# A decoder layer with routed experts: logits with experts on partitions, two shared blocks moved, scatters one by one

## The chip, the cores and the metric

The kernel runs on one core of a Trainium2 chip. The metric is the time on the device in microseconds, the median over the runs shown; lower is better. Beside it there is one execution with a profile, from which all durations of single instructions come. The core has five engines with a queue of instructions each: TensorE (PE; PEld is its weight load), VectorE (DVE), ScalarE (ACT), GpSimd (POOL) and SyncE (SP), which here only issues transfers. Each queue is worked off in order. Transfers run on 16 DMA engines.

## The reference

One decoder layer on x of 8 batches x 512 tokens x 256 features, in 32-bit floats, each part on the layer-normed x and added to x:

```python
x = x + _L0_attn_ref(_layernorm(x), W_A, W_V, W_O, b_O)          # 16 heads; a softmax over the tokens, applied as a causal convolution
x = x + _L0_xattn_ref(_layernorm(x), ctx_1024, ctx_1024, WK, WV, WQ)   # one causal head: softmax(Q K' / 16) V; K from x's norm, V and Q from ctx
x = x + _L0_ffn_ref(_layernorm(x), router_w, wg_r, wu_r, wd_r, wg_s, wu_s, wd_s)

# in _L0_ffn_ref, for each token t:
out = einsum(silu(t wg_s) * (t wu_s), wd_s)          # 2 shared experts, 128 wide
logits = flat @ router_w                             # 16 experts
weights, indices = top_k(softmax(logits), 2)         # weights scaled to sum 1
out = out + sum over the 2 chosen of weight * (silu(t wg_r) * (t wu_r)) wd_r    # routed experts, 64 wide
```

(The second part's arguments come in the order keys, values, queries.)

## The kernel before, in words

**Batches.** The loop over `b` handles one batch of 512 tokens at a time. Each batch has a front (`steps_front`: first norm, the token softmax `zsoft`, values, the context's queries and values), a back (`steps_back`: convolution `conv` and `summed`, output projection `proj`, second norm, `scores`, `probsT`, `attend`, third norm, router) and a shared block (`steps_shared`: two `hidden` with gate and up matmuls, two `down`). All are lists of small functions. `merged` (line 46) lays several lists over each other by the fraction of each list that a step stands at. In batch b run the back of b, the shared block of b-1 and the front of b+1.

**Order.** The order in which steps are called is the program order, and gives priorities. A planner then orders each engine's instructions, and puts a later one first where it expects the earlier to wait. So the trace shows the token column of batch 0's row tile (line 511) at 8.3 us, long before that batch's router. Tiles have tags with a fixed number of buffers (`bufs`); a tile waits until a buffer of its tag is free.

**Routing.** `router` (line 440) takes the transposed normed x (`x2T`) as the stationary operand against `wr_sb` with 16 columns, so that tokens lie on partitions and 16 logits beside each other, and VectorE finds the two best experts. `ranked` (line 487) counts tokens per expert with two matmuls and gives each a `place` in a table `xg` in DRAM; it also sets column 0 of the row tiles (line 511) to the number of the token's result row, r * n + token, where n is the number of tokens in the group. `send` (line 523) scatters the rows with indirect DMAs from GpSimd, 8 per batch of 129 KB. The tag `row` has two buffers, one for each of the two choices, so the next batch's row tiles wait for these scatters.

**Groups.** Batches 0 to 4 are group 0, batches 5 to 7 group 1. When a group's last batch is ranked, SyncE writes 17 blank blocks into `xg` (line 518), `tiled` and `tabled` make a table of row tiles, and the routed work (`steps_routed`) goes by four tiles of 128 rows, called q here: 14 q for group 0, 10 for group 1. For each q: `fetch` loads rows (`xs`) and down weights (`wdn`, two buffers) with register addresses on SyncE, `pick` copies gate and up weights on ScalarE, `turn` transposes the rows on TensorE (line 676), `hidden` (line 695) and `down` (line 709) are the expert, and its results `y`, weighted on ScalarE and VectorE (lines 720, 722), are scattered at once to `yg` by four indirect DMAs on GpSimd (line 723). GpSimd also does the small power of each layer norm (line 196).

Group 0's list of 72 steps is cut in three, 30, 30 and 12, laid over batches 5, 6 and 7. Group 1's list (`late`) runs after the batches, with the joins of group 0 laid over it. The shared block's end stores x as `kept` in DRAM (line 575); `keep`, `take` and `join` load it and the two result rows of each token (`yj`) back, add them (line 775) and store the output.

After batch 7's merged steps, router, `down` of block 6, `ranked`, the shared block of batch 7 and the sends come in a list written out by hand (line 810). The weight product `qk_sb` (wq times wk, line 159) is made before anything else on TensorE.

## Time and profile before

| | us |
|---|---|
| runs without profile | 666.7, 681.52, 676.43; median 676.43 |
| profiled execution, its own time | 669.43 |
| its span, first to last instruction | 667.7 |
| TensorE busy | 548.0 (82%) |
| VectorE busy | 376.3 (56%) |
| GpSimd busy | 227.8 (34%) |
| ScalarE busy | 187.6 (28%) |
| DMA moved | 109.77 MB, mean 164 GB/s |

The work stands in the trace as follows: batch 0 until about 90 us, then about 51 us a batch; batch 5 from 297 to 384, batch 6 to 474, batch 7 to 528 and its routing to 545; group 1's tiles from 564 to 638; scatters, joins and stores until the end. Busy time is summed over these stages, and a stage's own limit can differ from that of the whole. A wait line reads: engine and its waiting instruction, what released it, then total time, how often, and the longest. A timeline line reads: start, duration, engine, line, operation, output and inputs, count, and in brackets the engine's idle time before it with its releaser.

### The profile page before, as it was taken

Reading aid. Unit: us, or ns where it says so; the run is one execution under the profiler, and the core shown is the slowest. Engines: PE = TensorE matmul, PEld = TensorE weight load, DVE = VectorE, ACT = ScalarE, POOL = GpSimd, SP = SyncE. Lnnn points to the kernel's source line nnn. Section 1 sums busy time; section 2 is a strip of 40 time slices with the busy share of each in tenths; the row PEclk is TensorE's granted clock in tenths of the full one; section 3 lists DMA queues with packets and bytes.
Section 4 is the critical chain, followed back from the end, with each engine's and each line's share of the span. In section 5 each row is a group of like instructions: output and inputs, shape, how many; then the busy total and the mean of one; then the engine's idle time right before and its main releaser. Section 6 shows DMA issues by size and latency. Waiting matters only on the chain.

```text
span 667.7 us, 9943 instructions
## 1 busy us (share of the span) xinstructions
PE 548.0 (82%) x3132; PEld 346.1 (52%) x3132; DVE 376.3 (56%) x1213; ACT 187.6 (28%) x459; POOL 227.8 (34%) x257
## 2 busy tenths in 40 slices
PE   4879978998998998994999988999988881877820
PEld 2435624655655665552657645567565641654610
DVE  5156637668668658766455547554765481334424
ACT  2213212322322322312343332433422101433210
POOL 3011142125125125215033374325453521246560
PEclk9999988999999999999799998999989795979775
DMA  7562610631721631636338642286522077677879
GB/s 261 193 251 76 242 65 31 234 124 49 254 103 57 223 127 65 208 141 204 114 83 263 229 135 83 71 266 200 162 83 81 1 231 228 185 230 235 245 232 312
DMA packets 71397, 109.77 MB, mean 164 GB/s; under 512 B 9219, under 2 KB 45837, under 8 KB 70800
## 3 DMA queue, kind: packets, MB, share of 16 engines
q1 hardware_dynamic: 63664, 92.27, 43.0%
q0 software_dynamic: 7680, 16.87, 7.1%
q8 instruction: 25, 0.41, 0.3%
q14 instruction: 28, 0.23, 0.1%
HBM read 83.40 MB, written 35.43 MB: 178 GB/s over the span
## 4 chain that ended last, share of the span: by engine, by line
PE 46%; DMA 14%; DVE 12%; issue 10%; SPq 7%; POOL 7%; ACT 2%; POOLq 1%; DVEq 0%; ACTq 0%
DMA xs<-xg 5%; PE pa L419 4%; PE psc L390 4%; PE pt L212 4%; PE pv L306 3%; PE pv L276 3%; PE pq L294 3%; PE pgu L695 3%; PE pc L338 3%; PE pg L553 3%; POOL xg L527 3%; SPq L518 3%; POOL yg L723 2%; PE pz L244 2%; POOL rs L196 2%
## 5 line engine op out<-in xcount | busy, mean ns | idle before, releaser
L723 POOL DMA_INDIRECT yg<-y,to x96 | 97.7, 1018 | 113.8 <-ACT y L720 89.4
L196 POOL TENSOR_TENSOR rs<-ve,power 128x2 f32<-128x2 f32 x48 | 34.4, 723 | 167.0 <-DVE ve L195 166.9
L527 POOL DMA_INDIRECT xg<-row,place x64 | 63.1, 986 | 78.2 <-DVE place L510 50.6
L695 PE MATMUL pgu<-xsT,wgu 128*64 128x128 f32 x768 | 67.6, 316 | 7.5 <-ACT xsT L679 6.4
L695 PEld LDWEIGHTS pgu<-xsT,wgu 128*64 128x64 f32 x768 | 51.6, 158 | 23.7 <-issue 12.6
L676 PE MATMUL pxt<-ident,xs 128*128 128x128 f32 x192 | 37.6, 308 | 29.3 <-DMA xs<-xg 28.3
L338 PE MATMUL pc<-T,vh 128*32 128x256 f32 (+1 forms) x512 | 53.2, 493 | 9.0 <-DVE late L354 6.6
L676 PEld LDWEIGHTS pxt<-ident,xs 128*128 128x128 f32 x192 | 21.5, 148 | 49.7 <-DMA xs<-xg 30.2
L419 PE MATMUL pa<-v,pT 128*128 128x256 f32 x160 | 40.7, 385 | 2.8 <-DVE pT L410 2.8
L181 DVE BATCH_NORM_STATS2 bn<-x 128x6 f32<-128x256 f32 x96 | 38.0, 418 | 8.7 <-DMA x<-in_x_dram 7.6
L390 PE MATMUL psc<-kT,qT 128*128 128x128 f32 (+3 forms) x128 | 42.1, 460 | 0.5 <-ACT kT L215 0.5
L709 PE MATMUL py<-wdn,rh 64*128 64x256 f32 x192 | 37.5, 428 | 5.1 <-DVE h L557 4.7
L372 PE MATMUL po<-wo_sb,oT 128*128 128x256 f32 x128 | 35.1, 407 | 5.9 <-DVE oT L357 3.2
L200 DVE TENSOR_SCALAR xn<-x,mv,rs 128x256 f32<-128x256 f32 x64 | 26.5, 440 | 21.6 <-POOL rs L196 19.5
L212 PE MATMUL pt<-ident,xn 128*128 128x128 f32 x128 | 26.1, 302 | 15.1 <-DVE xn L200 11.6
L338 PEld LDWEIGHTS pc<-T,vh 128*32 128x32 f32 x512 | 16.3, 109 | 40.0 <-issue 24.5
L698 DVE SCALAR_TENSOR_TENSOR rh<-rh,pgu 128x256 f32<-128x256 f32 x24 | 10.0, 418 | 46.9 <-ACT rh L697 46.9
L663 ACT COPY wgu<-wgu_r 128x256 f32 x96 | 32.2, 401 | 11.6 <-DVE col L637 9.2
L570 PE MATMUL pd<-wd_sb,h 128*128 128x256 f32 x128 | 34.9, 411 | 0.5 <-DVE h L558 0.5
L306 PE MATMUL pv<-xwv_sb,ctxT 128*128 128x256 f32 x128 | 34.7, 392 | 0.0
L419 PEld LDWEIGHTS pa<-v,pT 128*128 128x128 f32 x160 | 29.2, 190 | 10.4 <-issue 3.7
L372 PEld LDWEIGHTS po<-wo_sb,oT 128*128 128x128 f32 x128 | 23.5, 197 | 20.7 <-issue 6.5
(156 smaller groups left out, 949.7 us busy)
## 6 DMA issues: line engine op xcount, KB each, us to landing
T<-zd SPq DMA_DIRECT2D x32, 1024.0 KB
xs<-xg SPq DMA_DIRECT2D x96, 129.0 KB
wdn<-wdn_d SPq DMA_DIRECT2D x96, 64.0 KB
xg<-blank SPq DMA_DIRECT2D x34, 129.0 KB
x<-in_x_dram SPq DMA_DIRECT2D x8, 512.0 KB
ctxT<-in_ctxT_dram SPq DMA_DIRECT2D x8, 512.0 KB
kept<-x SPq DMA_DIRECT2D x8, 512.0 KB
xj<-kept SPq DMA_DIRECT2D x8, 512.0 KB
```

The lines of the kernel that those rows point to most:

```text
L181: nc.vector.bn_stats(stats["bn"][:, c, :], src[:, c, :])
L196: nc.gpsimd.tensor_tensor(stats["rs"][:, lo:hi], ve[:, lo:hi], power[:, lo:hi], ALU.pow)
L212: nc.tensor.transpose(pt[:, i * P:(i + 1) * P], xn[:, k * P:(k + 1) * P], ident)
L306: nc.tensor.matmul(pv[:, i, :], s["ctxT"][:, k, j * P:(j + 1) * P], xwv_sb[:, k, :], start=(k == 0), stop=(k == KC - 1))
L338: nc.tensor.matmul(s["pc"][o][32 * g:32 * g + 32, 2 * jp * P:], v_bufs[b % 2][:, jp, h, :], s["T"][h // HPT][:, h % HPT, :S - 2 * jp * P], ...
L372: nc.tensor.matmul(po[:, i, :], s["oT"][:, k, c * P:(c + 1) * P], wo_sb[:, k, :], start=(k == 0), stop=(k == KC - 1))
L390: nc.tensor.matmul(pc[:, :w], s["qT"][:, k, i * P:w], s["kT"][:, k, :w], start=(k == 0), stop=(k == KC - 1))
L419: nc.tensor.matmul(pa[:, :D], s["pT", i][:, j * P:(j + 1) * P], s["v2"][:, j, :], start=(j == 0), stop=(j == i))
L527: ins = nc.gpsimd.indirect_dma_start(out=grp[g]["xg"][:, :], out_offset=bass.IndirectOffsetOnAxis(ap=s["place"][:, r, c:c + 1], axis=0), i ...
L676: nc.tensor.transpose(pt[:, i * P:(i + 1) * P], xs[:, i, 2 + k * P:2 + (k + 1) * P], ident)
L695: nc.tensor.matmul(p[o * MR:(o + 1) * MR, n, j, :], wgu[:, i, n, k, :], xT[:, k, i, :], start=(k == 0), stop=(k == KC - 1))
L723: ins = nc.gpsimd.indirect_dma_start(out=G["yg"][:, :], out_offset=bass.IndirectOffsetOnAxis(ap=G["to", q][:, i:i + 1], axis=0), in_=y[i], ...
```

## The change

The logits are made by a step `logits` of its own: `wr_sb`, padded with zeros to 32 columns, is stationary, and each group of 128 tokens goes to its own 32 partitions of the result. ScalarE copies it, and `router` transposes it back. `make_qk` moves behind batch 0's values. Shared block 5 moves whole from batch 6 to batch 7, and the two `hidden` of block 6 move to later places in batch 7. Group 0's list is spaced with empty steps (`idle`), and the scatters are steps of their own (`put`), one at a time between the other steps and two q later than the tile's `hidden`; group 1 scatters right after `down` as before. The list is now 152 steps, cut 72, 54, 26. The hand-written list at the end is in a new order, with the loads `keeps` and `takes` before `ranked`. Group 1's x is no longer stored in DRAM: it stays in its three buffers of tag `x`, and group 0's `keep` uses the buffers of `ctxT` and `oT` instead. The tags `xT`, `to` and `y` have 5, 4 and 8 buffers in place of 4, 3 and 5.

```diff
+def idle(n):
+    return [lambda: None] * n
...
-    wr_sb = load("wr_sb", wr, [P, KC, NE])
+    wr_sb = const.tile([P, KC, 32], F32, name="wr_sb")
+    nc.gpsimd.memset(wr_sb, 0.0)
+    nc.sync.dma_start(out=wr_sb[:, :, :NE], in_=wr)
...
-    for m in range(KC):
-        pq = ps.tile([P, 512], F32, tag="mm", bufs=3, name=f"pqk{m}")
...
+    def make_qk():
+        for m in range(KC):
+            pq = ps.tile([P, 512], F32, tag="mm", bufs=3, name=f"pqk{m}")
...
+        if b == 0:
+            steps.append(make_qk)
         steps += [queries(0), queries(1), context_values(0), context_values(1), bias]
...
+        def logits():
+            pl = ps.tile([P, 512], F32, tag="mm", bufs=3, name=f"pl{b}")
+            for k in range(KC):
+                for c in range(NT):
+                    nc.tensor.matmul(pl[32 * c:32 * c + 32, :P], wr_sb[:, k, :], s["x2T"][:, k, c * P:(c + 1) * P], start=(k == 0), stop=(k == KC - 1))
+            s["lT"] = sb.tile([P, P], F32, tag="lT", bufs=1, name=f"lT{b}")
+            nc.scalar.copy(s["lT"], pl[:, :P])
+
         def router():
-            pl = ps.tile([P, 512], F32, tag="mm", bufs=3, name=f"pl{b}")
-            pl3 = pl[:, :NT * NE].rearrange("p (c e) -> p c e", e=NE)
-            for c in range(NT):
-                for k in range(KC):
-                    nc.tensor.matmul(pl3[:, c, :], s["x2T"][:, k, c * P:(c + 1) * P], wr_sb[:, k, :], start=(k == 0), stop=(k == KC - 1))
+            pl = ps.tile([P, 512], F32, tag="tr", bufs=2, name=f"plt{b}")
+            nc.tensor.transpose(pl[:, :P], s["lT"], ident)
+            pl3 = pl[:, :P].rearrange("p (c e) -> p c e", e=32)[:, :, :NE]
...
-        steps += [router, ranked, send(0), send(1)]
+        steps += [logits, router, ranked, send(0), send(1)]
...
-                if cp == 1:
+                if cp == 1 and where[b][0] == 0:
                     s["kept"] = dram.tile([P, NT, D], F32, tag="kept", bufs=B, name=f"kept{b}")
...
-                        ins = nc.gpsimd.indirect_dma_start(
...
+                G["y", q] = y
+            return f
+
+        def put(q, i):
+            def f():
+                ins = nc.gpsimd.indirect_dma_start(
...
+            return f
...
-        steps += [lambda: tiled(g), lambda: tabled(g), fetch(0), fetch(1), pick(0), fetch(2), turn(0)] + [fetch(3)] * g
-        for q in range(nq + 1):
-            if q + 1 < nq:
-                steps += [pick(q + 1), turn(q + 1)]
-            if q < nq:
-                steps.append(hidden(q))
-            if q + 3 + g < nq:
-                steps.append(fetch(q + 3 + g))
-            if q > 0:
+        steps += [lambda: tiled(g), *idle(0 if g else 4), lambda: tabled(g), fetch(0), fetch(1), pick(0), fetch(2)]
+        steps += [fetch(3)] if g else idle(12)
+        steps.append(turn(0))
+        for q in range(nq + 2):
+
+            puts = [put(q - 2, i) for i in range(QT)] if g == 0 and q > 1 else idle(QT)
+            steps += [pick(q + 1), puts[0], turn(q + 1)] if q + 1 < nq else [puts[0]]
+            steps += [puts[1], hidden(q)] if q < nq else [puts[1]]
+            steps += [puts[2], fetch(q + 3 + g)] if q + 3 + g < nq else [puts[2]]
+            steps.append(puts[3])
+            if 0 < q <= nq:
                 steps.append(down(q - 1))
+                if g:
+                    steps += [put(q - 1, i) for i in (0, 2, 1, 3)]
...
-                x = sb.tile([P, NT, D], F32, tag="x", bufs=3, name=f"xj{b}")
+                x = sb.tile([P, NT, D], F32, tag=("ctxT", "oT")[bi % 2], bufs=1, name=f"xj{b}")
...
-                x, y = G["xj", bi], G["yj", bi]
+                x, y = G["xj", bi] if g == 0 else st[b]["x"], G["yj", bi]
...
-    n = len(routed) // 7
-    routed = [routed[:3 * n], routed[3 * n:6 * n], routed[6 * n:]]
+    first = [f for f in routed]
+    n = (len(first) - 18) // 14
+    routed = {5: first[:18 + 6 * n], 6: first[18 + 6 * n:18 + 12 * n], 7: first[18 + 12 * n:]}
+    shared = [steps_shared(b) for b in range(B)]
...
-        if b > 0:
-            now.append(steps_shared(b - 1))
+        if 0 < b < 6:
+            now.append(shared[b - 1])
...
-        if b >= 5:
-            now.append(routed[b - 5])
+        if b in routed:
+            now.append(routed[b])
         if b == B - 1:
 
-            router, ranked, *send = now[0][-4:]
-            hidden, down = now[1][:NSH], now[1][NSH:]
-            now[:2] = now[0][:-4], hidden
+            logits, router, ranked, *send = now[0][-5:]
+            now[0] = now[0][:-5]
+            now += [shared[5] + idle(3), idle(3) + shared[6][:NSH]]
...
-    for f in [router, *down, ranked, hidden[0], *send, late[0], keeps[0], takes[0], keeps[1], takes[1], hidden[1], late[1], *rest]:
+    for f in [logits, down6[0], router, keeps[0], takes[0], keeps[1], takes[1], down6[1], ranked, hidden7[0], *send, late[0], hidden7[1], late[1], *down7]:
         f()
     old = [joins[0], keeps[2], takes[2], joins[1], keeps[3], takes[3], joins[2], keeps[4], takes[4], joins[3], joins[4]]
-    keeps, takes, joins = steps_join(1)
-    for f in merged(late[2:], old):
+    _, takes, joins = steps_join(1)
+    for f in merged(late[2:], old + idle(4)):
         f()
-    for f in [*keeps, *takes, *joins]:
+    for f in [*takes, *joins]:
         f()
```

## The prediction

> **What bounds the kernel now.** I read the page first, then TensorE's waits between the batches' borders, then the timelines around the longest of them, then the chain after the last batch. From the page, busy tenths and granted clock in slices of 16.7 us, and one cost group:
>
> ```profile
> PE   4879978998998998994999988999988881877820
> ...
> PEclk9999988999999999999799998999989795979775
> ...
> L723 POOL DMA_INDIRECT yg<-y,to x96 | 97.7, 1018 | 113.8 <-ACT y L720 89.4
> ```
>
> TensorE is at 9 tenths in the batches, so a batch costs what TensorE has to do plus what it waits. Full waits are few. TensorE's waits in 295 to 320 us (batch 5 starts), 385 to 475 (batch 6) and 475 to 545 (batch 7):
>
> ```profile
> PE pxt L676 <- DMA xs<-xg: 6.1, 1, 6.1
> ...
> PE py L709 <- DVE h L557: 4.7, 1, 4.7
> ...
> PE pa L419 <- DVE pT L410: 2.8, 1, 2.8
> PE pt L212 <- DVE row L200: 2.2, 1, 2.2
> PE po L372 <- DVE oT L357: 2.0, 1, 2.0
> ```
>
> The first is the first transpose of routed rows, reached before its rows are. The other four lead to GpSimd. Its timeline at 390 us, and VectorE's:
>
> ```profile
> 389.10 0.97 POOL L723 DMA_INDIRECT yg<-y,to  x1 [0.31 <-DVE late L354]
> 390.38 0.96 POOL L527 DMA_INDIRECT xg<-row,place  x1 [0.30 <-DVE late L356]
> ...
> 399.21 0.96 POOL L527 DMA_INDIRECT xg<-row,place  x1 [0.30 <-issue]
> 400.18 0.73 POOL L196 TENSOR_TENSOR rs<-ve,power 128x2 f32<-128x2 f32 x1
> ...
> 400.95 0.73 DVE L200 TENSOR_SCALAR xn<-x,mv,rs 128x256 f32<-128x256 f32 x2 [8.78 <-POOL rs L196]
> ```
>
> Twelve scatters of about 1.27 us stand ahead of a layer norm's small power. VectorE waits 8.78 us for it, and the `h` of L557 that TensorE wants is queued behind. VectorE also stalls where the token column of the next row tile (L511) waits for the last batch's sends:
>
> ```profile
> 92.17 0.17 DVE L511 TENSOR_SCALAR row<-tok 128x4 f32<-128x4 f32 x1 [6.83 <-DMA xg<-row,place]
> ```
>
> After 545 us batches no longer count. The windows view gives TensorE 4.35 us of work in 545 to 565, and none after 638.3. The chain there runs blank rows, fetches on SyncE, scatters, loads of `yj`, two adds and the store.
>
> **The change, part by part** (against the span of 667.7 us; the execution's own time is 669.43, so 1.7 lie outside).
>
> 1. *`make_qk` goes behind the first values.* Now its 3.46 us (7.84 to 11.3) precede the first transposes, whose inputs are ready at 7.2 to 7.8: up to 3.5 us for the softmax chain. But TensorE waits only from 26.6 to 28.9 for `T` and 2.3 us more at 29 to 31, and the matmuls must still run before the queries. VectorE's wait for x1 until 11.8 can keep part. -2, from +0.5 to -3.5. The memset ahead of `wr_sb`'s load is hidden: GpSimd ends its constants at 2.3 us, that DMA is issued at 6.8.
>
> 2. *Logits.* Now 16 records per batch (L445) take 135.41 to 136.22, 137.67 to 137.89 and 138.40 to 139.02, together 1.65 us. After: 16 records moving 128 columns. The nearest row is L695 (128 columns, 64 wide), 32 records in 1.90 us, so 0.95; the transpose is 2 records of L212's kind (4 in 0.44), 0.22. TensorE saves 0.5 a batch. Against this stands the Trainium skill, "TensorEngine Tiling (Array Packing)", section "Restrictions": tiling by columns gives up the fast weight load. If the 16 loads then ran one after another at 109 ns (the row of L338, 128x32) it would be 1.75 us plus the transpose, 0.3 more than now instead of 0.5 less, 6.4 us over eight batches. L338 itself argues against: such tiles stream 48 records in 4.08 us (at 297.5), 85 ns each, below their 109 ns load, so the loads overlap. I take -0.5.
>  The added wait: copy on ScalarE (128x256 is 0.37, 128x128 about 0.3), transpose 0.2, and two handovers, some 0.2 each by the gaps between L212 and L215: VectorE starts the router about 1 us later, and `ranked`, the sends and L511 with it. Queued behind L511 are `late`, `oT` and TensorE's `po`. Five borders show that stall. The transposed logits also hold one of two `tr` buffers until the router's subtraction, 0.5 us. Eight times -0.5 is -4; five times +1 is +5: +1, from -4 to +8 (the transpose queued behind other matmuls, rival C).
>
> 3. *Head of group 0 in batch 5.* Twelve empty steps put `turn(0)` at 22.5/72 of the batch instead of 6.5/30: 0.10 of 87 us, 8 us later, more than the 6.1 us waited. The attention of batch 5 fills the place. The cold clock behind the wait goes too. In rows: 8 `pxt` in 2.17 us (1.04 at 482 us), 4 `pt` 1.12 (0.60), 32 `pgu` 3.68 (1.97), 4 `pg` 2.12 (1.88) sum to 3.6 us lost; the windows view gives a clock of 0.51 from 317.2 to 325. The Trainium skill, "TensorE: Matmul & The Clock Gate", section "Part 1: The HAM clock gate", allows one window of about 3.4 us at half rate after an idle one, a loss of 1.7. By the rule this part is worth 7.8, by the rows 9.7, because the clock stayed low over twice that time. Rows decide; but six tiles now turn in batch 5 instead of five, over less of it, and a fetch may be awaited again (now 2.2 us). -8, from -2 to -10.
>
> 4. *Scatters one by one, two tiles late; shared blocks.* 24 and 20 scatters stay at 1.27 us each. What goes is GpSimd waiting for `y` (89.4 us in the group above), and four in a row ahead of a power. The eight sends stay in a row, but start when `place` is ready (387 instead of 390.4; 477.2 instead of 480.1), so L196, L511 and their followers come 3 us or more earlier. Of the waits 4.7 + 2.8 + 2.2 + 2.0 = 11.7 I take -8, from 0 to -11.7. The moved blocks are neutral in work: 16 gate/up and 16 down records (4 in 1.72, 8 in 1.73 us) of block 5 leave batch 6 for batch 7, 10.3 us (block 6's gate and up are there already), and one routed tile of about 5 us moves ahead over each of the borders 5/6 and 6/7. They cost where tag `h` has three buffers: both `h` of block 5 now are held at 1.5/7 when `summed(1)` at 5.5/24 wants two. The shuffle then waits for `down` of block 5, and `oT`, `proj` and the attention of batch 7 behind it. TensorE has the 7 us of the block itself and routed tiles to do meanwhile: +2, from 0 to +6. A fifth `xT` buffer and eight `y` buffers cost only space.
>
> 5. *Dispatch of group 1.* From the first router step (531.49) to `both` (539.5) VectorE takes 8.2 us; in batch 1 5.1 (139.20 to 144.3). Between them stand two adds of `down` with waits of 0.56 and 1.61. These go around the router now: -3, and +1 for the longer logits. The loads of `keeps` and `takes` go ahead of `ranked`, so beside 17 blank loads (11.2 us of SyncE) there is no `yj` and no `kept` store; the last blank's 5.62 us of landing should come nearer 4.6 as in group 0: -1. Together -3, from -5 to +1.
>
> 6. *Late tiles, 564 to 638.* Ten tiles at 7.4 us. `wdn` has two buffers, so SyncE issues tile q's only when `py` of q-2 is done (576.46, issue at 576.48), then `xs` of q+1 (1.9), which lands in some 3 us, and that sets `py` of q. Old joins sit in this queue: out 0.59, xj 0.58, two yj 1.2. By step positions there are ten instead of nine ahead of the last fetch, and `keep` 4 reuses the buffer of join 2 just ahead of it: +0.6 and up to a landing of 3, less contention: +2, from -3 to +7.
>
> 7. *End.* No `xj` loads for group 1 (issued at 634.7, 642.8 and 649.8) and joins of group 0 over earlier: a scatter took 7.33 us to land at 633, 2.1 later, and held the next by 1.5; 512 KB at 262 GB/s is 2 us beside the `yj` loads. -3, from 0 to -5.
>
> Sum: -2 + 1 - 8 - 8 + 2 - 3 + 2 - 3 = -19: span 648.7, execution 650.4. The median shown is 676.43/669.43 = 1.0105 times the profiled one: 657.
>
> **Rivals.**
> *B, waits move.* Removing one stall exposes the next: VectorE and the fetches also have gaps in batches 5 to 7 (`xs` is awaited at 363 and 421 in the chain), so half of part 3 and a third of part 4 come through: -2 + 1 - 4 - 3 + 2 - 1 + 2 - 2 = -7, 660.7, median 669. For: nearly every wait of VectorE there is short and has another behind it. Against: TensorE is at 0.93 to 0.96 in those batches, so it has work ready.
> *C, slower: the transpose of the logits waits in TensorE's queue behind shared gate and up* (3.8 us, at 139.5 to 143.1 just there now). Seven borders at 3.8 are 27, and 2 more at the last: -19 + 29 = +10, 677.7, median 686. It decides from 19/7 = 2.7 us of extra delay per border. Against: the planner places these fillers where it expects a wait, so it may as well place the transpose first.
> *D, more:* all waits of parts 3 and 4 and the late contention go: 644.
>
> **Numbers.** Forecast 0.55 (650 to 664), B 0.25, C 0.10, D 0.10. Runs of before spread from 666.7 to 681.5, so 2% (662.9) is what can be told from no change. Faster: 0.48 + 0.03 + 0.09 = 0.60; slower: half of C, whose median lies just inside 2%, and a remainder, 0.05 + 0.04 = 0.09; same 0.31. The range reaches to B's upper and D's near end: 644 to 678, leaving out most of C and the far half of D.
>
> **What would show it.** First `pxt` with no wait and clock 1.0 from 310 to 340 (3); no L200 waiting over 3 us for L196 in batches 6 and 7 (4); first transposes near 8 us and `T` issued before 22 (1); L511's waits longer by about 1 us in batches 1 to 4 (2); 32 us from the first router step of batch 7 to the first late `pgu`, now 35.1 (531.49 to 566.61) (5); tiles of 7.4 to 7.7 us (6); at most 27 us from last `py` to end, now 29.4 (7). I am wrong if the router's chain lengthens by over 2 us a batch, or if batch 6 keeps its 90 us without its shared block.

## The result and the profile after

The changed kernel takes 679.86 us (median of 20 runs, 674.14 to 684.23). The kernel before, run beside it on the same chip, takes 674.46 us. The ratio is 1.010, with a 95% interval from 1.0067 to 1.0133: a little slower, where 657 us and "faster" were forecast. The profiled execution of after is near the slow end of its runs (span 681.0 us) and that of before near the fast end of its own (667.7), so the two profiles differ by 13.3 us where the medians differ by 5.4. So sizes of totals are taken from the ratios, and a stage of a single profile is read with care: e10, e11, e12 and e15 differ only in batches 5 to 7, and their batch 0 takes 81.4 to 84.3 us, their batches 1 to 4 together 214.5 to 218.1.

From the page of after, the busy tenths and the clock in slices of 17.0 us, and the costliest group:

```profile
PE   4878978999899889899799897999989780687930
...
PEclk9999989999899899799799997989979985788575
...
L746 POOL DMA_INDIRECT yg<-y,to x96 | 95.4, 994 | 113.8 <-ACT y L738 87.3
```

TensorE is as full as before. What stands out is the last line: the wait of GpSimd for `y`, which was to go when the scatters became steps of their own, is 87.3 us; it was 89.4 (line 723 of the kernel before). The clock row has lost a tenth or two in several places of the first half.

Where the time lies is read by stages. Stage b0 runs from the start to the first count matmul (`pk`) of batch 0, and a stage b1 to b7 from the first `pk` of the batch before to the first `pk` of its own. "Dispatch" goes from batch 7's `pk` to the first transpose of group 1's rows, "late" to the end of the last `py`, and "end" to the end of the span. All rows of this table are profiles from chips on which before takes 674 to 675 us:

| us | b0 | b1 | b2 | b3 | b4 | b5 | b6 | b7 | dispatch | late | end | span |
|---|---|---|---|---|---|---|---|---|---|---|---|---|
| before | 82.9 | 61.5 | 50.5 | 51.3 | 50.8 | 87.2 | 89.7 | 66.5 | 23.7 | 74.2 | 29.4 | 667.7 |
| after | 85.6 | 64.6 | 54.2 | 54.8 | 56.1 | 82.2 | 85.1 | 75.3 | 23.5 | 72.9 | 26.7 | 681.0 |
| e13 | 84.5 | 65.2 | 54.3 | 54.7 | 54.5 | 83.4 | 85.7 | 61.7 | 20.2 | 78.8 | 27.9 | 671.0 |
| e14 | 82.5 | 63.9 | 51.4 | 51.8 | 51.5 | 88.6 | 85.8 | 75.0 | 23.4 | 73.5 | 26.9 | 674.3 |
| e9 | 82.4 | 63.9 | 51.4 | 51.8 | 51.5 | 88.8 | 86.7 | 61.3 | 19.9 | 82.4 | 27.4 | 667.4 |
| e15 | 82.4 | 63.4 | 52.3 | 51.5 | 50.9 | 87.4 | 88.1 | 62.3 | 20.0 | 79.9 | 26.8 | 664.9 |
| e10 | 84.3 | 61.8 | 50.7 | 51.7 | 50.9 | 96.6 | 87.0 | 64.1 | 19.6 | 80.7 | 26.7 | 674.2 |
| e11 | 82.8 | 61.7 | 50.8 | 51.1 | 52.0 | 89.1 | 90.9 | 58.7 | 20.1 | 82.7 | 28.1 | 668.2 |
| e12 | 81.4 | 61.4 | 51.2 | 51.2 | 50.8 | 96.6 | 90.4 | 58.6 | 20.5 | 79.7 | 28.0 | 669.8 |
| e16 | 82.0 | 63.8 | 51.2 | 52.0 | 51.6 | 88.3 | 90.1 | 60.5 | 21.8 | 82.0 | 26.9 | 670.3 |
| e17 | 83.2 | 65.2 | 52.2 | 54.0 | 53.8 | 85.3 | 92.5 | 61.9 | 19.8 | 85.8 | 26.8 | 680.6 |
| e18 | 81.4 | 61.8 | 50.8 | 51.2 | 51.9 | 89.2 | 87.1 | 63.8 | 19.5 | 84.0 | 26.7 | 667.4 |

After loses 2.7 us in batch 0 and 3.1 to 5.3 us in each of the batches 1 to 4, where the forecast saw almost nothing, wins 5.0 and 4.6 in batches 5 and 6, and loses 8.8 in batch 7. The end is 2.7 us shorter. (The lower rows are the experiments told below.)

The long waits answer to those shown before. TensorE's waits in batch 5, in batch 6 and in batch 7 of after, the longest of each:

```profile
PE pt L221 <- DVE xn L209: 3.5, 1, 3.5
...
PE po L383 <- DVE oT L368: 3.1, 1, 3.1
...
PE pt L221 <- DVE row L209: 3.4, 1, 3.4
```

The wait of 6.1 us for the first routed rows is gone, and so are `py` for `h` and `pa` for `pT`. In their places stand three waits of 3 us and more. GpSimd's timeline at the border of batches 5 and 6 shows why the one in batch 6 stays:

```profile
398.78 0.97 POOL L746 DMA_INDIRECT yg<-y,to  x1 [0.31 <-DVE run L518]
400.06 0.97 POOL L545 DMA_INDIRECT xg<-row,place  x1 [0.30 <-DVE place L528]
...
408.92 0.96 POOL L545 DMA_INDIRECT xg<-row,place  x1 [0.30 <-issue]
410.19 0.99 POOL L746 DMA_INDIRECT yg<-y,to  x1 [0.30 <-issue]
...
414.05 0.97 POOL L746 DMA_INDIRECT yg<-y,to  x1 [0.30 <-issue]
415.03 0.75 POOL L205 TENSOR_TENSOR rs<-ve,power 128x2 f32<-128x2 f32 x1
```

Four scatters from 394.9 to 399.8, eight sends, four scatters, and then the norm's small power: sixteen indirect DMAs of 1.27 us in one row. VectorE's waits in 397 to 562 us of after show what that costs:

```profile
DVE xn L209 <- POOL rs L205: 7.5, 4, 6.1
```

The longest, 6.1 us, ends with the power at 415.8 (it was 8.78), and `oT`, which TensorE's `po` at 418.3 needs, stands behind it in VectorE's queue. The scatters are steps of their own in the list, but the planner puts them where `y` and GpSimd are ready, and that is again together.

### The profile page after: what moved, and what is told of

It reads as the page before. It is cut to its first block, busy times and chain, and to the rows that moved or that the text cites. A ratio compares the mean times of both kernels' runs of the same rounds, so it can differ in the third digit from the quotient of the medians.

```text
span 681.0 us, 9957 instructions
## 1 busy us (share of the span) xinstructions
PE 554.5 (81%) x3140; PEld 337.6 (50%) x3140; DVE 371.1 (54%) x1213; ACT 189.1 (28%) x467; POOL 227.5 (33%) x258
## 4 chain that ended last, share of the span: by engine, by line
PE 43%; DVE 15%; DMA 12%; issue 12%; POOL 8%; SPq 6%; ACT 3%; POOLq 0%; DVEq 0%; ACTq 0%
PE pgu L713 6%; PE pt L221 4%; PE pa L430 4%; DMA xs<-xg 3%; PE psc L401 3%; POOL rs L205 3%; PE pq L303 3%; PE pg L571 3%; DMA xg<-row,place 3%; PE py L727 3%; PE pc L349 3%; POOL yg L746 2%; PE pu L571 2%; PE pv L315 2%; PE pz L253 2%
## 5 line engine op out<-in xcount | busy, mean ns | idle before, releaser
L746 POOL DMA_INDIRECT yg<-y,to x96 | 95.4, 994 | 113.8 <-ACT y L738 87.3
L545 POOL DMA_INDIRECT xg<-row,place x64 | 63.8, 997 | 92.1 <-DVE place L528 64.8
L713 PE MATMUL pgu<-xsT,wgu 128*64 128x128 f32 x768 | 62.9, 309 | 7.9 <-ACT xsT L697 7.9
L713 PEld LDWEIGHTS pgu<-xsT,wgu 128*64 128x64 f32 x768 | 50.1, 154 | 22.7 <-ACT xsT L697 10.9
L694 PE MATMUL pxt<-ident,xs 128*128 128x128 f32 x192 | 35.2, 307 | 24.9 <-DMA xs<-xg 24.5
L221 PE MATMUL pt<-ident,xn 128*128 128x128 f32 x128 | 28.9, 328 | 27.5 <-DVE xn L209 23.4
L694 PEld LDWEIGHTS pxt<-ident,xs 128*128 128x128 f32 x192 | 23.4, 153 | 41.4 <-issue 24.7
L401 PE MATMUL psc<-kT,qT 128*128 128x256 f32 (+3 forms) x128 | 42.7, 466 | 1.2 <-ACT kT L224 1.2
L430 PE MATMUL pa<-v,pT 128*128 128x256 f32 x160 | 41.0, 387 | 1.9 <-DVE pT L421 1.8
L383 PE MATMUL po<-wo_sb,oT 128*128 128x256 f32 x128 | 37.9, 427 | 4.6 <-DVE oT L368 3.1
L221 PEld LDWEIGHTS pt<-ident,xn 128*128 128x128 f32 x128 | 15.9, 158 | 49.9 <-issue 21.3
L727 PE MATMUL py<-wdn,rh 64*128 64x256 f32 x192 | 40.0, 436 | 0.4 <-PE py L727 0.4
L716 DVE SCALAR_TENSOR_TENSOR rh<-rh,pgu 128x256 f32<-128x256 f32 x24 | 10.0, 418 | 51.8 <-ACT rh L715 51.6
L430 PEld LDWEIGHTS pa<-v,pT 128*128 128x128 f32 x160 | 29.5, 192 | 14.2 <-issue 6.6
L349 PEld LDWEIGHTS pc<-T,vh 128*32 128x32 f32 x512 | 16.4, 111 | 40.5 <-issue 23.5
```

What stands on the lines that cost most here:

```text
L221: nc.tensor.transpose(pt[:, i * P:(i + 1) * P], xn[:, k * P:(k + 1) * P], ident)
L349: nc.tensor.matmul(s["pc"][o][32 * g:32 * g + 32, 2 * jp * P:], v_bufs[b % 2][:, jp, h, :], s["T"][h // HPT][:, h % HPT, :S - 2 * jp * P], ...
L383: nc.tensor.matmul(po[:, i, :], s["oT"][:, k, c * P:(c + 1) * P], wo_sb[:, k, :], start=(k == 0), stop=(k == KC - 1))
L401: nc.tensor.matmul(pc[:, :w], s["qT"][:, k, i * P:w], s["kT"][:, k, :w], start=(k == 0), stop=(k == KC - 1))
L430: nc.tensor.matmul(pa[:, :D], s["pT", i][:, j * P:(j + 1) * P], s["v2"][:, j, :], start=(j == 0), stop=(j == i))
L545: ins = nc.gpsimd.indirect_dma_start(out=grp[g]["xg"][:, :], out_offset=bass.IndirectOffsetOnAxis(ap=s["place"][:, r, c:c + 1], axis=0), i ...
```

## The experiments

Three things are unlike before at once in the stages that lose: the back's list has 29 steps instead of 28 (`logits` is a step), the logits themselves are made in another way, and group 0's joins have another place. Each kernel is timed against before on the same chip in the same series. In the first two series before takes 709 to 712 us, in the others 674 to 675. Ratios are compared only within a series or between series of one speed; a difference of two of them is uncertain by 0.3 to 0.5%, and in the second series by more.

### First series: the step and the logits, one at a time

e1 is the kernel before with one empty step ahead of every router:

```diff
-        steps += [router, ranked, send(0), send(1)]
+        steps += [lambda: None, router, ranked, send(0), send(1)]
```

> The kernel before with one empty step put into every batch's back list, ahead of the router: 29 steps in place of 28, no instruction added or removed. Theory A (place): the extra step shifts how the lists are laid over each other, so that the queries of the next batch come after the fourth transpose of the probabilities, and TensorE waits in mid-batch: batches 0 to 4 take 12 to 18 us longer in all, as in the kernel after (first count matmul of batch 4 at 309 to 315 us in place of 297), and the whole is about 2% slower, 685 to 692. Theory B (the new logits cost it): no difference, within 0.5%.

Measured: 717.01 against 709.14 us, 1.0112 [1.0086, 1.0139]. A step that computes nothing costs about 1.1%: more than theory B allows and about half of what theory A forecast.

e2 is the kernel before with the new logits, called inside `router`, so 28 steps:

```diff
         def router():
+            logits()
```

> The kernel before with the new logits (experts on partitions, copy, transpose) called inside the router's own step, so that the list keeps 28 steps. Theory A: batches 0 to 4 change by no more than 3 us in all, the whole within 1% of before. Theory B: batches 0 to 4 take 12 us or more longer, 685 us or more.

Measured: 711.56 us, 1.0054 [1.0014, 1.0093]. The new logits cost about half a per cent without the step, in theory A's range.

e3 is the changed kernel with `logits()` called inside `router` in this way (28 steps).

> The kernel after with logits and router in one step (28 steps). Theory A: the loss of 12 to 18 us in batches 0 to 4 goes, 662 to 668 in all, faster than before by 1 to 2%. Theory B: as the kernel after, 680.

Measured: 721.7 us, 1.0144 [1.0072, 1.0217], from 4 runs. The gain that theory A expected isn't there.

e4 is the changed kernel with the router of before (28 steps).

> The kernel after with the router of before (logits with tokens on partitions, one step, 28 steps). Theory A: as with the new logits in one step, within 1% of it. Theory B: faster than that by 12 us or more.

Measured: 719.7 us, 1.0137 [1.0111, 1.0163]. Taking part 2 back doesn't bring the changed kernel below before: something from batch 5 on costs too. In e4's stages batch 7 is the long one, 88.4 us.

### Second series: the joins of group 0

On VectorE's timeline of after, the stretch between the last batch's third norm and its router:

```profile
537.08 0.18 DVE L191 BATCH_NORM_AGGREGATE mv<-bn 128x2 f32<-128x6 f32 x1
540.73 1.22 DVE L804 TENSOR_TENSOR xj<-xj,yj_qT 128x1024 f32<-128x1024 f32 x1 [3.47 <-DMA yj_qT<-yg]
541.87 0.16 DVE L204 TENSOR_SCALAR ve<-mv 128x2 f32<-128x2 f32 x1
541.94 0.68 DVE L590 TENSOR_TENSOR x<-pd,x 128x512 f32<-128x512 f32 x1
542.88 0.73 DVE L209 TENSOR_SCALAR row<-x,mv,rs 128x256 f32<-128x256 f32 x2 [0.26 <-POOL rs L205]
543.53 1.22 DVE L804 TENSOR_TENSOR xj<-xj,yj_v 128x1024 f32<-128x1024 f32 x1
...
550.09 0.23 DVE L475 TENSOR_REDUCE r<-plt 128x4 f32<-128x64 f32 x1 [3.28 <-PE plt L462]
```

L804 is the join of group 0. Its first add stands ahead of the norm's epsilon (L204, 0.16 us) and waits 3.47 us for the loaded result rows; the norm, `row` and TensorE's `pt` wait behind it, and that is the 3.4 us of the last wait line shown above. Three adds of 1.22 us are done before VectorE's first router step at 550.09, and a fourth goes right behind it. In the kernel before, `keep` needed buffers of tag `x`, which came free late: its first join add is at 540.35, behind the last step of the router (539.5). Now the joins use `ctxT` and `oT`, which the last batch leaves early. The list calls all joins after `ranked`; the planner draws them forward.

e5 is the changed kernel again, as the base of the series, and e8 the kernel before, for its trace.

> The kernel after, unchanged, beside its variants on one chip. Theory A (the loss is the extra step in batches 0 to 4, and the joins of group 0 in batch 7): slower than before by about 1%, and its batches 0 to 4 longer than in the kernel before of this job by 5 us or more. Theory B (the routed steps and the moved shared block cost it): batches 0 to 4 equal within 3 us, and the loss lies in batches 5 to 7.

> The kernel before, unchanged, one look for a profile on the same chip. Theory A: its batches 0 to 4 take 5 us or more less than those of the kernel after on this chip, and batch 7 to the first late tile 8 us less. Theory B: batches 0 to 4 within 3 us.

Measured: e5 733.53 against 712.45 us, 1.037 [1.0264, 1.0477], from 4 runs; e8 708.56 us in its one execution. Here the change costs over twice what it costs in the comparison above, so its loss isn't one number.

e6 is the changed kernel with the adds held behind the last batch's `place`:

```diff
-                nc.vector.tensor_copy(place[:, r], spot)
+                s["place_ins"] = nc.vector.tensor_copy(place[:, r], spot).ins
...
-                for r in range(2):
-                    nc.vector.tensor_tensor(x, x, y[r], ALU.add)
+                with tc.issue_after(st[B - 1]["place_ins"]):
+                    for r in range(2):
+                        nc.vector.tensor_tensor(x, x, y[r], ALU.add)
```

> The kernel after, with one edit: the adds of group 0's joins are queued behind the last batch's place on VectorE, so that none of the eight adds (1.22 us each) that were ahead of it in the kernel after stays there. Theory A: batch 7 to the first late tile 8 to 12 us shorter, late tiles up to 6 us longer, in all 3 to 8 us faster than the kernel after. Theory B: no more than 2 us faster, since the adds fill gaps of VectorE.

Measured: 725.21 us, 1.0211 [1.0123, 1.0299], from 4 runs. Batch 7 goes from 86.5 to 76.6 us and the dispatch from 26.1 to 20.1; the late tiles, which now run beside all the joins, go from 79.2 to 83.6.

e7 is e6 with the router of before (28 steps).

> As the last, and with the router of before too (28 steps). Theory A: faster than the kernel before by 0.5 to 1.5%. Theory B: within 0.5% of the last or slower than before by 0.5% or more.

Measured: 710.67 us, 0.9996 [0.9969, 1.0023]. Part 2 and its step are worth 2.1% in this series. The joins come to 1.6%, but with four runs of e5 and of e6 that is uncertain by 1.4. Together they are the whole loss there.

### Third and fourth series: the causes at the first speed

I had taken from e1 to e6 that step and logits cost little by themselves in batches 1 to 4 and much together. e9, e13, e14 and e15 test this in four combinations. e9 is e3 with the joins held as in e6, e13 is e6 once more, e14 is e3 and e15 is e7 once more.

> The changed kernel with logits and router in one list step (28 steps, not 29) and with group 0's joins held behind the last batch's place on VectorE. Theory (the added step and the new logits cost 3.5 us a batch only together, because the step shifts the merged order): 1.000 to 1.005 of before, batches 1 to 4 at about the period of before (within 0.7 us). Rival (the logits with experts on partitions cost it by themselves): 1.014 to 1.021, as the changed kernel with the joins held (1.021).

> The changed kernel with only the joins of group 0 held behind the last place (29 steps). Theory (the step costs 3.5 us in each of batches 1 to 4, and the joins some 1.5%): 1.5 to 2.2% above e9, so 1.010 to 1.017 on a chip where before takes about 675 us, and 0 to 0.5% under the changed kernel's 1.010 only if the late tiles give back what batch 7 gains. Rival (the step costs nothing once the joins are held, and e9's gain is the chip's): within 0.4% of e9.

> The changed kernel with logits and router in one step (28), joins not held. Theory (the joins in VectorE's queue ahead of the last router and ranked cost 1 to 1.9%): 1.004 to 1.014 of before. Rival (the joins cost only where the step has lengthened the batches): 0.993 to 0.998, as e9.

> e7 again, beside the others: changed kernel, router of before (28 steps), joins held. Theory (new logits are worth nothing to speak of without the step): within 0.4% of e9, 0.991 to 0.999. Rival (the new logits themselves gain TensorE time): over 0.4% above e9, 0.999 to 1.004.

Measured:

| kernel | logits | steps | joins | us | ratio |
|---|---|---|---|---|---|
| after | new | 29 | early | 679.86 | 1.010 [1.0067, 1.0133] |
| e13 | new | 29 | held | 674.12 | 1.0021 [0.9995, 1.0046] |
| e14 | new | 28 | early | 675.35 | 1.0017 [0.9989, 1.0044] |
| e9 | new | 28 | held | 670.19 | 0.9947 [0.9926, 0.9968] |
| e15 | old | 28 | held | 665.46 | 0.989 [0.9864, 0.9916] |

With the new logits, the step costs 0.83% with the joins early and 0.74% with the joins held; the joins cost 0.79% with the step and 0.70% without. So within the uncertainty these two add up, and the rivals of e13 and e14 (each matters only beside the other) fall. Both are smaller than their theories had them: e13 was expected 1.5 to 2.2% above e9 and is 0.74, e14 at 1.004 or more and is 1.0017. e9 itself came out below its theory. Without the step the new logits cost 0.57%, which e15's theory had at nothing and its rival as a gain: neither came true.

In the stages the step is 2.9 to 3.0 us in each of b2 to b4 (e13 against e9). e13 loses some 12 us to e9 in batches 0 to 4, and its batches 5, 6 and late tiles give 10 of them back; the total, 0.74% or 5 us by the ratios, is what is left of both. The windows view of one stretch of batch 3, from batch 4's first `pz` to batch 3's first `pk`, gives for e13, e9 and e15 the window, its length, the busy time (and records) of PE, PEld, DVE, ACT and POOL, the clock, the share of the DMA engines and GB/s:

```profile
226.65:258.85 32.20, 30.39 (x125) 18.11 (x124) 18.71 (x71) 8.60 (x21) 4.61 (x7) 0.97 0.53 181
```

```profile
219.95:249.50 29.55, 28.84 (x125) 17.80 (x124) 18.94 (x71) 8.54 (x22) 4.83 (x7) 1.00 0.59 197
```

```profile
220.75:249.65 28.90, 28.90 (x124) 18.91 (x123) 18.88 (x71) 8.30 (x21) 4.86 (x7) 1.00 0.60 202
```

For the same 125 records e13 takes 2.65 us more than e9: 1.55 of busy time, at a lower clock, and 1.10 of waiting. TensorE's timeline of e13 shows both:

```profile
226.69 1.89 PE L253 MATMUL pz<-xnT,wa_sb 128*16 128x512 f32 x2
...
235.61 1.03 PE L430 MATMUL pa<-v,pT 128*128 128x256 f32 x4
236.47 1.89 PE L285 MATMUL pv<-wv_sb,xr 128*128 128x256 f32 x8
238.20 0.93 PE L418 MATMUL ppt<-ident,pr 128*128 128x128 f32 x7
239.86 0.33 PE L221 MATMUL pt<-ident,row 128*128 128x128 f32 x1 [0.73 <-ACT pT L423]
240.55 1.56 PE L430 MATMUL pa<-v,pT 128*128 128x256 f32 x6 [0.37 <-DVE pT L421]
```

The same place in e9:

```profile
219.97 1.03 PE L253 MATMUL pz<-xnT,wa_sb 128*16 128x512 f32 x2
...
229.59 1.03 PE L430 MATMUL pa<-v,pT 128*128 128x256 f32 x4
230.45 0.49 PE L418 MATMUL ppt<-ident,pr 128*128 128x128 f32 x3
230.78 1.88 PE L303 MATMUL pq<-ctxT,qk_sb 128*128 128x512 f32 x4
232.50 1.46 PE L430 MATMUL pa<-v,pT 128*128 128x256 f32 x6
233.79 0.60 PE L418 MATMUL ppt<-ident,pr 128*128 128x128 f32 x4
```

In e9, `queries` (L303) and `attend` (L430) lie between the seven transposes of the probabilities (`ppt`, L418), and ScalarE and VectorE have their copies done meanwhile. With 28 steps `merged` gives the order `probsT(2)`, `queries(0)`, `attend(2)`, `probsT(3)`, `queries(1)`. With 29 each back step stands at another fraction, and it is `probsT(2)`, `attend(2)`, `queries(0)`, `probsT(3)`. Nothing then stands between `probsT(2)` and the `attend` that needs its copy, and in the trace the planner has drawn the four transposes of `probsT(3)` forward: all seven come in one go, followed by what needs their copies, 0.73 and 0.37 us. `queries(0)` comes after the waits that it covered in e9.

In this stretch the new logits add 0.65 us (e9 against e15). TensorE's timeline of e9 has after the last `attend`:

```profile
239.93 0.41 PE L456 MATMUL pl<-x2T,wr_sb 128*32 128x128 f32 x2
241.04 0.41 PE L221 MATMUL pt<-ident,row 128*128 128x128 f32 x2 [0.71 <-DVE row L209]
```

and that of e15:

```profile
240.64 0.96 PE L454 MATMUL pl<-wr_sb,x2T 128*128 128x16 f32 x8
```

The old loop goes over tokens outside and over the two halves of the features inside, so eight records can run on the first half of the tokens, and they fill the time in which VectorE makes the other half of `row`. The new loop goes over features outside: at most four can run, two did, and TensorE waits 0.71 us. Its busy time is the same within 0.06 us. That the loop order is the reason is read from these lines; the other order of the new loop wasn't tried.

Batches 1 to 4 together, over all profiles at this speed, confirm both sizes. With 28 steps and the old logits they take 214.0 to 218.1 us (before, e10, e11, e12, e15, e18; mean 215.5), with 28 steps and the new logits 218.5 to 218.7 (e9, e14, e16), with 29 steps and the old logits 225.3 (e17, told below), with 29 and the new 228.8 and 229.6 (e13, after). So here the new logits are worth some 3 us and the step some 10. e15 is the slowest of its six, so e9 against e15 alone shows 0.4 of these 3 us.

The third and fourth series also took back two edits of parts 3 and 4 of the change. e10 is e15 with `turn(0)` ahead of the twelve empty steps, e11 is e15 with shared block 5 back in batch 6, e12 is both, and e16 is e9 with the block back in batch 6. The edits are

```diff
-        steps += [fetch(3)] if g else idle(12)
+        steps += [fetch(3)] if g else []
         steps.append(turn(0))
+        steps += [] if g else idle(12)
```

and

```diff
-        if 0 < b < 6:
+        if 0 < b < 7:
...
-            now += [shared[5] + idle(3), idle(3) + shared[6][:NSH]]
+            now.insert(1, shared[6][:NSH])
```

> Like e7 (changed kernel with the router of before and the joins held, 0.9996), but with the first turn of group 0 ahead of the twelve empty steps, so about where it was. Theory (the later head brought batch 5 some 5 us that nothing took back): first late tile of group 0 waits again for its rows, 1.006 to 1.008. Rival (the rest of batches 5 and 6 is bound by the chain of GpSimd and VectorE, and the wait is only moved): 0.998 to 1.002.

> Like e7, but with the shared block of batch 5 back in batch 6 instead of batch 7. Theory (batch 6 isn't bound by TensorE's work, as it stayed at 94 to 97 us without its block, so the block fits there in waits): batch 6 longer by at most 3 us, batch 7 shorter by 5 to 8, 0.990 to 0.996. Rival (batch 7 hides the block in its own waits; moving it is neutral): batch 6 longer by 8 to 10 us or both unchanged, 0.998 to 1.006.

> Both edits at once: of the changed kernel there remain the late qk, the scatters as own steps with eight y buffers, five xT buffers, x of group 1 kept in SBUF, takes ahead of ranked, joins held. If the two edits add up: the product of the two ratios over 0.9996. Theory: 0.996 to 1.003. Rival (the twelve steps were needed because the block had left batch 6, so with the block back they bring nothing): equal to the run with the block alone, within 0.003.

> e9 with the shared block of batch 5 back in batch 6: of the changed kernel without the added step, joins held. Theory (the block fits into the waits of batch 6, 2 to 4 us longer, and batch 7 is shorter by 2.5 to 5): 0.988 to 0.994, the fastest of all. Rival (moving the block is neutral, as batch 6 pays what batch 7 gains): 0.993 to 0.997.

Measured: e10 672.56 us, 0.9999 [0.9964, 1.0034]; e11 670.18, 0.9939 [0.9906, 0.9972]; e12 675.83, 1.0015 [0.9989, 1.0041]; e16 672.29, 1.002 [0.9982, 1.0058].

The ratios that the expectations take for e15 came from the slower series (0.9996); e15 itself is 0.989 here, so e10 and e11 are read against that. The late head is worth 1.1% (e10 against e15). It lies in batch 5, 96.6 against 87.4 us. TensorE's timeline of e10 has these two waits for routed rows:

```profile
319.22 1.17 PE L685 MATMUL pxt<-ident,xs 128*128 128x128 f32 x4 [5.54 <-DMA xs<-xg]
...
372.18 0.66 PE L685 MATMUL pxt<-ident,xs 128*128 128x128 f32 x2 [5.65 <-DMA xs<-xg]
```

and that of e15 the second alone:

```profile
365.41 2.39 PE L685 MATMUL pxt<-ident,xs 128*128 128x128 f32 x8 [5.17 <-DMA xs<-xg]
```

The theory of e10 stands, at a larger size. Moving the block is worth 0.5% (e11 against e15) and 0.7% (e16 against e9). The theory of e11 and e16, that the block belongs in batch 6, falls by the total (e16 is outside both of its ranges), though its reading of batch 6 holds: with the block's matmuls back, 10.3 us by the prediction's estimate, batch 6 is only 2.8 and 3.4 us longer. TensorE's longest wait in batch 6 shows it. In e15:

```profile
PE po L381 <- DVE oT L364: 6.7, 1, 6.7
```

In e11:

```profile
PE py L718 <- DVE h L566: 2.0, 1, 2.0
```

The block filled that wait. Batch 7 pays 3.6 us for it (e15 against e11) and 0.8 (e9 against e16); where in the rest of the span the gain of the total lies is not settled, as the stages there differ by 1 to 3 us from kernel to kernel. e12, with both edits, is above either alone: the head brings 1.25 - 0.49 = 0.76% with the block in batch 6, and 1.09% with it in batch 7.

### Fifth series: the fourth combination, and the weight product

e17 is e15 with the empty step (old logits, 29 steps); e18 is e15 with `make_qk()` called at its old place.

> e15 (changed kernel, router of before, joins held) with one empty step ahead of the router in every batch: 29 steps, no new logits. Theory (step and logits each cost 0.6 to 0.8%, whichever goes first): 0.995 to 0.999 of before. Rival (the step costs only together with the new logits, whose records then no longer fill a wait): 0.987 to 0.992, as e15.

> e15 with qk made ahead of the first transposes, as in the kernel before. Theory (moving it brought 0.5 us, as the first context transpose came 0.4 us earlier): within 0.2% of e15, 0.987 to 0.991. Rival (it brought the 2 us forecast): 0.991 to 0.994.

Measured: e17 678.97 us, 1.0107 [1.0079, 1.0135]; e18 668.54, 0.9861 [0.9808, 0.9913] from 6 runs; before 673.57.

e17 answers outside both expectations. The step costs 2.2% with the old logits (against e15) and 0.74% with the new. In the windows view of the same stretch of batch 3, e17 is

```profile
223.00:254.70 31.70, 30.60 (x124) 19.24 (x123) 18.52 (x71) 8.34 (x20) 4.59 (x7) 0.96 0.54 184
```

2.80 us above e15, with the same two waits of 0.7 and 0.4 us: in this stretch the step costs the same with either router, and over batches 1 to 4 about the same. My reading of the first series, that the two cost only together, doesn't hold at this speed. In the slower series the profiles do show it: batches 1 to 4 take 225.2 to 229.3 us with the old logits and 28 steps (e8, e4, e7) and 229.6 with 29 (e1), against 227.8 and 228.7 with the new logits and 28 (e2, e3) and 239.9 with 29 (e5, e6). The rest of e17's loss lies in batch 6 (92.5 against 88.1 us) and the late tiles (85.8 against 79.9), where e13 shows none of it; e17's profiled execution is 3.3 us above the median of its runs, which is part of it. Why the step costs there with the old logits alone is open. One thing follows for the account: beside the step the new logits are a gain (e13 is 0.86% below e17), without it a cost (0.57%), so only the two together, 1.3% (e13 against e15), are a size that doesn't depend on the order in which one takes them back.

e18 leaves the 2 us open that the late weight product was to bring. Its recorded ratio lies on e15's or below it, but the plain ratio of the medians, 668.54 / 673.57 = 0.993, lies in the rival's range, and six runs can't tell 0.3%.

## Why the prediction was wrong

The forecast was -19 us. At the first speed the runs give this account, in per cent of 674 us: the changed kernel +1.0 (7 us); of it the step and the new logits together 1.3 (9 us), where part 2 had +1 us, and the joins 0.7 to 0.8 (5 us), which no part had. What is left over, e15, is -1.1 (7 us faster than before), where the other parts had -20. So about half of the miss is these costs, and half are gains that didn't come, in parts 3 and 4 above all. By the numbered parts:

1. **`make_qk` behind the values**: forecast -2. The first transposes moved from 11.13 to 7.36 us, as foreseen, but the first `T` load was issued only 0.45 us earlier (22.15 against 22.60 us), so the sign "before 22" failed. Batch 0 alone varies by 3 us between kernels that are alike there, and e18 is too uncertain, so what this part brought in all is open. Of the two waits for `T` that the part named only the first is in the trace, 2.29 us until 28.89; from 29 to 31 us TensorE is busy throughout.

2. **Logits**: forecast +1, and here it failed. The step priced matmuls and the border: TensorE 0.5 us less a batch, the router 1 us later. Neither was what counted, and the second didn't come: from the last transpose of `row` to VectorE's first router step it is 2.08 us in before and 2.04 in after, in each of batches 0 to 4. From the first shared gate matmul (`pg`) to `pk`, batch 3 takes 4.83 us in before, e9, e13 and e15 alike, so rival C (the transpose waiting behind these) cost nothing. Two things were not in the sum. `logits` is one more entry in the back's list, and `merged` goes by fractions, so every step of the back moved: 2.9 to 3.0 us in each of batches 2 to 4 in e13 against e9, about a third of it waits and the rest a lower clock. I priced the twelve empty steps of part 3 by just this rule and didn't apply it to the step of part 2. And the new logits took away records that covered a wait: 0.65 us in batch 3, and some 3 us in batches 1 to 4, where -0.5 a batch was forecast. The Trainium skill's rule on the fast weight load ("TensorEngine Tiling (Array Packing)", section "Restrictions"), weighed in that part, shows no cost: TensorE's busy time is the same within 0.06 us.

3. **Head of group 0**: forecast -8. The mechanism and its size were right: the first `pxt` of after has no wait, and against the same kernel without the lateness it brings 9.2 us (e10 to e15) and 7.5 us (e12 to e11) in batch 5. But it was counted from the batch 5 of before, and the rest of the new list isn't neutral there: e10, with the turn at its old place, has a batch 5 of 96.6 us instead of 87.2. Two terms were missing. One is the clock and the waits that come in place of the first: in after the clock is 1.00 from 310 to 330 us and 0.66 from 330 to 340, with a new wait of 3.5 us for `xn` that ends at 332.9. The other is a later fetch. The forecast had "a fetch may be awaited again (now 2.2 us)" and gave it no price; e10 and e15 wait 5.65 and 5.17 us for rows at 372 and 365 us, where before waits 1.25. After itself waits 1.81 there, does 192 records of `pgu` in batch 5 instead of 160, and is 5.0 us shorter, so of the forecast 8 some 5 came. Why the later fetch is awaited longer with 28 steps (5.2 to 6.3 us in e9, e14, e15 and e16) than with 29 (1.8 to 3.2 in after, e13 and e17) is open.

4. **Scatters and shared blocks**: forecast -6. "What goes is GpSimd waiting for `y`" failed: 87.3 us instead of 89.4, and four scatters still stand in a row ahead of a power, with a wait of 6.1 us where the sign allowed 3. VectorE's waits for the power in the stretch of batches 6 and 7 went from 19.0 to 11.5 us in all, so the mechanism exists in part. "The moved blocks are neutral in work" failed as well: the block had been filling a wait in batch 6. Without it the batch shrank by 4.6 us, not by 10 and more, and its clock fell from 0.98 to 0.94. (In the total the move still gains, 0.5 to 0.7% by e11 and e16, where the forecast had a cost of 2 us.) That was the sign set down beforehand: "if batch 6 keeps its 90 us without its shared block". It kept 85.

5. **Dispatch of group 1**: forecast -3. It came to -0.2 in after and to -3.5 and -3.8 in e13 and e9, once the joins were held. So the price was right and the joins took it. They cost more in batch 7, 13.6 us by the stages of after and e13, of which the late tiles give back 5.9. This is the second step of the forecast that failed: the adds of group 0's joins were put at nothing, and they cost 0.7 to 0.8% (5 us). The forecast asked where the loads of the joins go, and not where their adds go once their buffers come free early.

6. **Late tiles**: forecast +2; -1.3 in after, and +4.6 to +8.2 in e13, e9 and e15, where all joins run beside them.

7. **End**: forecast -3, measured -2.7.

Of the rivals, B ("waits move") describes batches 5 and 6 of after best: `pxt` gave way to `pt`, and `py` to `po`. C had the sign, but not by its mechanism. None of them had the lengthened list, the covered wait and the early joins, which decided the sign.

## What to carry to other kernels

Where lists of steps are merged by fractions, a new entry moves all others of its list: price it by reading what will stand next to what, above all between a producer's burst and its readers, and call a new operation inside an existing step where nothing speaks for a step of its own. When a change frees a buffer, ask which instructions become ready early and which in-order queue they will then stand in; here a join that nobody was waiting for held up the router, and one ordering edge on its adds took back 0.7 to 0.8%, and 1.6 (uncertain by 1.4) in the slower series. The kernel that combines both lessons (e15: router of before, joins held, the rest of the change) takes 0.989 [0.9864, 0.9916] of before, so in that series it is faster than before and after; in the slower series it is level with before.

## What was not expected of the hardware

**The clock can depend on where the waits fall.** Before batch 4's `pz`, TensorE waits in e13 and e9 at the same places and for nearly the same time (2.3 us for `xn` in both). The windows view of e13 then shows

```profile
224.00:226.50 2.50, 1.38 (x6) 0.69 (x6) 2.07 (x8) 1.30 (x5) 1.20 (x1) 0.80 0.00 0
226.50:229.00 2.50, 2.50 (x7) 0.60 (x5) 0.44 (x2) 0.89 (x2) 1.15 (x1) 0.52 0.50 208
```

and that of e9

```profile
218.00:220.50 2.50, 1.64 (x8) 0.58 (x7) 2.05 (x7) 1.70 (x7) 1.67 (x1) 1.00 0.00 0
220.50:223.00 2.50, 2.50 (x9) 0.91 (x8) 1.15 (x3) 0.46 (x1) 0.87 (x2) 1.00 0.51 210
```

If the low rate is half (the `pz` pairs above take 1.89 us in e13 and 1.03 in e9), the first ran (0.20 + 0.48) x 2.5 / 0.5 = 3.4 us at it, and the second none. The Trainium skill, "TensorE: Matmul & The Clock Gate", section "Part 1: The HAM clock gate", states windows of about 3.4 us that run freely; a single one at half rate is just what the two rows add up to. That the two kernels differ in how their waits fall into such windows would explain it, but no run here shows it. Nor does it hang on the step alone: batch 2 of e15, with 28 steps, has a clock of 0.97 and 49.8 us of busy time, batch 2 of e17, with 29, has 1.00 and 48.7.

**One kernel ran at two speeds, and not by a factor alone.** Before takes 674 us in some series and 709 to 712 in others. The changed kernel is 1.010 of before at the one and 1.037 at the other, e14's 1.0017 and 1.0144, e15's 0.989 and 0.9996. The series ran on different chips, but the second and the fourth, 712 and 674 us, carry the same chip number in the record, so whether the chip or something else sets the speed is not shown. A gain of half a per cent found in one series says little of another.
